# Softmax sums gathered by a chain of accumulating transfers, division on VectorE, and a new order at the start of each round

## The chip, the cores and the metric

The kernel runs on one core of a Trainium2 chip. The metric is the device time of one execution in microseconds (us). The engines are named as in the profile: PE is TensorE's matmul (PEld its weight load), DVE is VectorE, ACT is ScalarE, POOL is GpSimd, SP is SyncE.

## The reference

One transformer layer in float32 on `x` of 2 x 2048 x 512: a layer norm, attention with 16 query heads of 32 columns that share 2 key and value heads, and a linear layer in FP8. Cut to what matters here:

```python
x = x + attention(layernorm(x))
x = x + fp8_linear(layernorm(x), w_ffn)

def attention(x):
    q, k, v = x @ wq + bq, x @ wk + bk, x @ wv + bv   # 16, 2 and 2 heads of 32 columns
    q, k = rotary(q), rotary(k)
    scores = einsum('bqhd,bkhd->bhqk', q * hd**-0.5, repeat(k)) * hd**-0.5
    attn = softmax(scores, axis=-1)
    return einsum('bhqk,bkhd->bqhd', attn, repeat(v)).reshape(b, s, d) @ wo + bo
```

The softmax is exact: for each query and head the kernel needs the largest score, the sum of the exponentials over 2048 keys, and the values weighted by the exponentials, which are divided by that sum.

## The kernel before, in words

The tokens form 8 blocks of 512. A block's 16 heads are taken four at a time (a quad), and a quad's 512 queries in two halves of 256. One quad and half is a **unit**; there are 64, numbered `u`. The main loop runs over units, and in each over four **rounds** of four key chunks (128 keys each). In the text rounds are numbered 1 to 4 (`r` is 0 to 3 in the code).

Each round does two things at once. For the next unit it computes plain scores (`s`, queries on partitions, L517) and their maxima over the keys (DVE's reductions into `part`, L524). For this unit it computes transposed scores `T` (keys on partitions, L963; in round 1 the maxima come in ahead of them by the selector matmuls of L954), from which ACT makes the exponentials `p` (L972), and PE multiplies these with the values (`columns`, L913) into `avs[:, 0, :]`. Plain scores come in pairs, one for each call of `next(scores)`. The text calls the four pairs of a round a, b, c and d. PE's order in a round is: a, T of the first and second chunk, b, other work, T of the third, c, T of the fourth, other work, d, then the value matmuls of all four chunks, and in some rounds sums behind them.

PSUM has eight banks in use. Two tiles of two banks (`E` and `O`) hold `T` by turns. Three banks hold `s`, of which one is lent to other work (projections, output products, transposes) while such work is going on. One bank holds the tile `avs`: its first half are the weighted values of this unit, its second half the sums of the unit before.

The sums of the exponentials are made in two steps. On POOL `add_pair` (L946) adds the exponentials of two chunks; the round's first pair goes to a tile `pair`, its second to a tile of `far_sums`, and an accumulating transfer from POOL's queue (L1015) adds the first to the second. In round 3 one more transfer (L1017) adds the far sum of round 1 to that of round 2. So three tiles are left, and PE adds these over the partitions with a matrix of ones (`sum_up`, L927) into `avs[:, 1, :]` in the next unit: two tiles behind the values of round 1, one behind those of round 2. Each tile takes eight of the instructions that the profile counts.

Then `finish_heads` divides: ACT copies the sums from PSUM to the SBUF tile `both` (L885), DVE takes the reciprocals in two pieces (L889), and POOL multiplies them with the values (L890), which ACT had copied from `avs[:, 0, :]` to `both` at the unit's end (L1033).

Each engine works through its queue in the order in which the kernel writes it down. Around the fixed steps, `fill` hands out pieces of other work at set places: PE's pieces behind b and behind the fourth T, DVE's behind d. A list `finishing` goes ahead of the lists `queue` and `beside`. What a kind of step waits for is settled when the program is built: an instruction waits for a count of the engine or the transfer that it depends on.

Of the kernel before, what the change touches and what calls it, by code (L numbers as in the profile page):

```python
# [8 lines left out]
F32 = mybir.dt.float32  # L9
# [4 lines left out]
ALU = mybir.AluOpType  # L14
AX = mybir.AxisListType

P = 128
# [10 lines left out]
def preln_attn_fp8_ffn_kernel(  # L28
# [37 lines left out]
    nc = tc.nc  # L66
# [9 lines left out]
    HB = 256  # L76
# [6 lines left out]
    ON_PE, ON_DVE, OTHER = "PE", "DVE", "other"  # L83
# [9 lines left out]
    w2 = ctx.enter_context(tc.tile_pool(name="w2", bufs=6))  # L93
# [376 lines left out]
    units = [(k, half) for k in range(len(quads)) for half in range(HALVES)]  # L470
# [20 lines left out]
    def batch(k):  # L491
        return quads[k][0] // NB
# [267 lines left out]
    finishing = []  # L760
    attn_of = {}

    def fill(kind, pieces=1):

        for _ in range(pieces):
            ready = [job for job in queue if job.due <= step[0] and not job.waits()]
            if lent[0] is not None:
                ready = [job for job in ready if job is owner[0]]
            able = [
                (jobs, job)  # L770
                for jobs, some in ((finishing, finishing[:1]), (queue, ready), (beside, beside))
                for job in some
                if job.kind in (kind, OTHER) and job.due <= step[0]
            ]
            if able:
                do(*able[0])

    def do(jobs, job):
        held = lent[0]
        job.step()  # L780
        if held is None and lent[0] is not None:
            owner[0] = job
        if job.kind is None:
            jobs.remove(job)
# [93 lines left out]
            fetch_y_over_keys(4, "kS", 0)  # L878
            fetch_y_over_keys(5, "dkS", 0)

    def finish_heads(u, both, sums):

        k, half = units[u]
        n, quad = quads[k]
        nc.scalar.copy(both[:, 1, :], sums)  # L885
        for c in range(HB // P):
            yield ON_DVE
            piece = both[:, 1, c * P : (c + 1) * P]
            nc.vector.reciprocal(piece, piece)  # L889
        nc.gpsimd.tensor_tensor(  # L890
            attn_of[n][:, quad, half * HB : (half + 1) * HB], both[:, 0, :], both[:, 1, :], ALU.mult
        )
        if n == NBLK - 1:
            if quad == QUADS - 2 and half == HALVES - 1:
                queue.append(Job(finish_most(n, x_res[n], attn_of[n])))
            elif quad == QUADS - 1:
                queue.append(Job(finish_rest(n, x_res[n], attn_of[n], half)))
        elif quad == QUADS - 1 and half == HALVES - 1:
            job = Job(finish_block(n, attn_of.pop(n)))
            if n not in biased:  # L900
                job.due = NEVER
                without_x[n] = job
            queue.append(job)

    def columns(u, chunks, probs, av):

        k, half = units[u]
        for kc, p in zip(chunks, probs):
            if kc == NTS - 2 and u + 1 < len(units):
                tp = ps_t.tile([P, 4 * HB], F32, tag="E", name=f"mtp_{u + 1}")  # L910
                gather_maxima(u + 1, tp)
            for j in range(4):
                nc.tensor.matmul(  # L913
                    av[j * HD : (j + 1) * HD, :],
                    vX[batch(k)][:, kc, group(k), :],
                    p[:, j, :],
                    start=(kc == 0),
                    stop=(kc == NTS - 1),
                    tile_position=(0, j * HD),
                    skip_group_check=True,  # L920
                )

    def sum_up(dst, parts, start, stop):

# [12 lines left out]
    def add_pair(u, kc, a, b):  # L937
        far = kc % ROUND == 2
        pa = papool.tile(
            [P, 4, HB],  # L940
            F32,
            tag="pa" if far else "pair",
            name=f"pa_{u}_{kc}",
            bufs=4 if far else 2,
        )
        nc.gpsimd.tensor_tensor(pa, a, b, ALU.add)  # L946
        return pa

    def probabilities(u, T, kc):

        k, half = units[u]
        if kc < 2:
            for j in range(4):
                nc.tensor.matmul(  # L954
                    T[:, j, :],
                    sel[:, j, :],
                    maxima[u],
                    start=(j % 2 == 0),
                    stop=True,
                    skip_group_check=True,  # L960
                )
        for j in range(0, 4, 2):
            nc.tensor.matmul(  # L963
                T[:, j : j + 2, :],
                stacked["dkS"][:, group(k), kc * P : (kc + 1) * P],
                qst[k][:, j : j + 2, half * HB : (half + 1) * HB],
                start=False,
                stop=True,
                skip_group_check=True,
            )  # L970
        p = ppool.tile([P, 4, HB], F32, tag="p", name=f"p_{u}_{kc}")
        nc.scalar.activation(p, T, AF.Exp, scale=SCALE)  # L972
        return p

    with tc.manual_schedule():
        for _ in range(LEAD):
            next(scores)
        for u, (k, half) in enumerate(units):
            n, quad = quads[k]
            if half == 0 and quad == 0:  # L980
                attn_of[n] = wide.tile(
                    [P, QUADS, TB], F32, tag="attn", name=f"attn_{n}", bufs=2
                )
            stack_next(u)
            banks = [
                ps_t.tile([P, 4, HB], F32, tag="EO"[parity], name=f"T_{u}_{parity}")
                for parity in range(2)
            ]

            far_sums = []  # L990
            whole = u == len(units) - 1
            ending_soon = u >= len(units) - 2
            pieces = 2 if ending_soon else 1
            for r in range(ROUNDS):
                chunks = list(range(r * ROUND, (r + 1) * ROUND))
                step[0] += 1
                while r == 1 and landing:
                    landing.pop()()
                if r == 2:
                    ask(u)  # L1000
                last = r == ROUNDS - 1
                next(scores, None)
                probs = [probabilities(u, banks[kc % 2], kc) for kc in chunks[:2]]
                pair = add_pair(u, chunks[0], *probs)
                next(scores, None)
                if r > 0:
                    fill(ON_PE, pieces)
                probs.append(probabilities(u, banks[0], chunks[2]))
                next(scores, None)
                probs.append(probabilities(u, banks[1], chunks[3]))  # L1010
                if ending_soon:
                    fill(ON_DVE)
                if not (last and whole):
                    far_sums.append(add_pair(u, chunks[2], *probs[2:]))
                    nc.gpsimd.dma_start(out=far_sums[r], in_=pair, accum_op=ALU.add)  # L1015
                if r == 2:
                    nc.gpsimd.dma_start(out=far_sums[1], in_=far_sums[0], accum_op=ALU.add)  # L1017
                fill(ON_PE, pieces)
                next(scores, None)
                split_maxima()  # L1020
                fill(ON_DVE, 3 if finishing else 2)
                if r == 0:
                    avs = ps_av.tile([P, 2, HB], F32, tag="av", name=f"avs_{u}")
                columns(u, chunks, probs, avs[:, 0, :])


                if u > 0 and r == 0:
                    sum_up(avs[:, 1, :], far_before[1:3], False, False)
                elif u > 0 and r == 1:
                    sum_up(avs[:, 1, :], far_before[3:], False, True)  # L1030
                    finishing.append(Job(finish_heads(u - 1, both, avs[:, 1, :])))
            both = w2.tile([P, 2, HB], F32, tag="both", name=f"both_{u}", bufs=1)
            nc.scalar.copy(both[:, 0, :], avs[:, 0, :])  # L1033
            far_before = far_sums
        sums = ps_s.tile([P, TB], F32, tag=s_bank(), name="sums_last")[:, :HB]
        sum_up(sums, [pair, *probs[2:], *far_sums[1:]], True, True)
        finishing.append(Job(finish_heads(u, both, sums)))
        fetch_y_over_keys(2, "kS", 1)
        attending[0] = False
        for jobs in (finishing, queue, beside):  # L1040
            while jobs:
                jobs[0].step()
                if jobs[0].kind is None:
                    jobs.pop(0)
# [122 lines left out]
```

## Time and profile before

| | |
|---|---|
| median of 3 runs | 2333.02 us (2332.41 to 2335.74) |
| profiled execution, its own time | 2336.02 us |
| its span, first to last instruction | 2334.2 us |
| mean granted clock of TensorE | 0.97 |
| busy: PE, DVE, ACT, POOL | 92%, 73%, 53%, 76% |
| main loop, about 130 to 2215 us | 64 units of 28.3 to 41.5 us |
| rounds in it | mostly 6.8 to 9.4 us |
| accumulating transfers between SBUF tiles | 319 of 512 KB, 4.9 us to landing (median) |

The span has three parts: the projections of the first blocks (to about 130 us), the main loop, and the FP8 layer (from about 2235 us). A group's line gives the instructions' count, then busy time and mean ns of one, then the idle time of the engine just before them and what ended it. A line of the timeline gives start, length, engine, line, what is written and read, and in brackets how long the engine was idle before and who ended that. Where a line says "x4", four instructions are merged.

### The profile page before, as it was taken

The numbers are of one execution on the slowest core, as the hardware profiler recorded it, in microseconds if no ns is written. First come the engines' busy times: TensorE is split into PE (matmuls) and PEld (weight loads), VectorE is DVE, ScalarE is ACT, GpSimd is POOL, SyncE is SP. The second block draws the span as 40 slices with busy tenths as digits, with TensorE's granted clock in tenths as the row PEclk, the third lists the DMA queues.
The fourth block names the chain that finished last, engine by engine and source line by source line (L and its number), as shares of the span: only waits on it lengthen the run. The fifth ranks groups of instructions, "written<-read, shape, count | busy, mean of one in ns | idle before, by whom it ended". The sixth has DMA issues, their size and how long they took to land. (4 is left out here: it accounts for less than half of the span.)

```text
span 2334.2 us, 39403 instructions
## 1 busy us (share of the span) xinstructions
PE 2143.7 (92%) x15506; PEld 1242.2 (53%) x15506; DVE 1698.0 (73%) x2679; ACT 1237.0 (53%) x1545; POOL 1765.1 (76%) x1199
## 2 busy tenths in 40 slices
PE   5499999999999999999999999999999899899955
PEld 3255555555555555555555555555555455555522
DVE  3467778776777776876767778676877977767578
ACT  2146556655556555655445456555555555545646
POOL 3268889888878987888868878887888777877810
PEclk9599999999999999999999999999999999999978
DMA  6546656666465765659586456664665645847512
GB/s 204 160 102 128 141 114 161 140 142 131 100 163 130 159 129 136 145 115 197 103 202 137 102 127 136 147 112 96 133 154 123 138 101 115 170 98 197 109 52 112
DMA packets 116411, 312.78 MB, mean 134 GB/s; under 512 B 16896, under 2 KB 17536, under 8 KB 112384
## 3 DMA queue, kind: packets, MB, share of 16 engines
q0 software_dynamic: 50160, 175.66, 40.0%
q1 hardware_dynamic: 63648, 133.21, 19.2%
q8 instruction: 122, 2.00, 0.3%
q10 hardware_dynamic: 2416, 1.38, 0.2%
q14 instruction: 65, 0.53, 0.1%
HBM read 91.56 MB, written 42.99 MB: 58 GB/s over the span
## 5 line engine op out<-in xcount | busy, mean ns | idle before, releaser
L524 DVE TENSOR_REDUCE part<-s 128x1 f32<-128x512 f32 x2048 | 1304.2, 684 | 541.8 <-PE s L517 528.8
L946 POOL TENSOR_TENSOR pa<-p,p 128x1024 f32<-128x1024 f32 x511 | 1234.9, 2466 | 293.1 <-ACT p L972 265.8
L972 ACT ACTIVATE p<-T 128x1024 f32<-128x1024 f32 x1024 | 1001.4, 1024 | 597.8 <-PE T L963 564.6
L517 PE MATMUL s<-kS,qst 128*128 128x512 f32 x2048 | 832.1, 465 | 87.6 <-DVE part L524 28.7
L963 PE MATMUL T<-qst,dkS 128*128 128x512 f32 x2048 | 669.5, 423 | 11.8 <-ACT p L972 11.8
L517 PEld LDWEIGHTS s<-kS,qst 128*128 128x128 f32 x2048 | 369.7, 190 | 478.0 <-DVE part L524 266.5
L913 PE MATMUL avs<-p,vX 128*32 128x256 f32 x8192 | 509.4, 383 | 0.8 <-ACT p L972 0.8
L963 PEld LDWEIGHTS T<-qst,dkS 128*128 128x128 f32 x2048 | 366.0, 189 | 159.8 <-ACT p L972 54.8
L913 PEld LDWEIGHTS avs<-p,vX 128*32 128x32 f32 x8192 | 233.1, 109 | 214.4 <-issue 79.6
L1015 POOL DMA_DIRECT2D pa<-pa x255 | 224.2, 879 | 80.3 <-POOL pa L946 75.6
L301 PE MATMUL po<-wo_sb,attn 128*128 128x512 f32 x256 | 130.7, 596 | 1.3 <-POOL attn L890 1.3
L889 DVE RECIPROCAL both<-both 128x128 f32<-128x128 f32 x128 | 112.4, 920 | 11.2 <-ACT both L885 11.2
L301 PE MATMUL pq<-xnT_q,wq_sb 128*128 128x512 f32 x224 | 114.3, 592 | 0.0
L927 PE MATMUL avs<-pa,ones 128*32 128x256 f32 x1512 | 105.5, 382 | 5.5 <-DMA pa<-pa 5.5
L885 ACT COPY both<-avs 128x256 f32<-128x256 f32 x63 | 23.5, 372 | 132.8 <-PE avs L927 132.8
L890 POOL TENSOR_TENSOR attn<-both 128x256 f32<-128x256 f32 x64 | 85.2, 1331 | 5.9 <-DVE both L889 5.9
L954 PEld LDWEIGHTS T<-mT,sel 128*128 128x128 f32 x512 | 78.7, 190 | 13.6 <-ACT mT L546 1.9
L954 PE MATMUL T<-mT,sel 128*128 128x256 f32 x512 | 82.2, 283 | 1.1 <-ACT mT L546 1.1
L1017 POOL DMA_DIRECT2D pa<-pa x64 | 74.2, 1159 | 3.9 <-DMA pa<-pa 3.6
L927 PEld LDWEIGHTS avs<-pa,ones 128*32 128x32 f32 x1512 | 49.2, 111 | 38.6 <-DMA pa<-pa 6.0
L546 ACT CAST mT<-mtp 128x256 fp32r<-128x256 f32 x64 | 23.9, 373 | 84.0 <-PE mtp L542 84.0
L532 ACT CAST mrow<-mx 128x8 fp32r<-128x8 f32 x64 | 13.1, 205 | 93.5 <-DVE mx L531 93.5
(126 smaller groups left out, 1160.8 us busy)
## 6 DMA issues: line engine op xcount, KB each, us to landing
pa<-pa POOLq DMA_DIRECT2D x319, 512.0 KB, 4.9
qst<-q_far SPq DMA_DIRECT2D x128, 256.0 KB, 4.3
x_kv<-in_L_attn_x_dram SPq DMA_DIRECT2D x8, 1024.0 KB, 8.8
q_far<-hi_q SPq DMA_DIRECT2D x32, 256.0 KB, 4.4
q_far<-lo_q SPq DMA_DIRECT2D x32, 256.0 KB, 3.7
x_res<-in_L_attn_x_dram SPq DMA_DIRECT2D x8, 1024.0 KB, 8.2
x_res<-in_L_attn_bo_dram POOLq DMA_DIRECT2D x8, 1024.0 KB, 11.6
out_dram<-v SPq DMA_DIRECT2D x16, 512.0 KB, 2.8
```

What stands on the lines that cost most here:

```text
L301: nc.tensor.matmul(dst, lhs(c), rhs(c), start=(c == 0), stop=(c == chunks - 1))
L517: nc.tensor.matmul(s, qst[k][:, j, at : at + P], stacked["kS"][:, group(k), kb * TB : (kb + 1) * TB], start=True, stop=True,)
L524: nc.vector.tensor_reduce(part[:, i, j, kb : kb + 1], s, AX.X, ALU.max)
L889: nc.vector.reciprocal(piece, piece)
L890: nc.gpsimd.tensor_tensor(attn_of[n][:, quad, half * HB : (half + 1) * HB], both[:, 0, :], both[:, 1, :], ALU.mult)
L913: nc.tensor.matmul(av[j * HD : (j + 1) * HD, :], vX[batch(k)][:, kc, group(k), :], p[:, j, :], start=(kc == 0), stop=(kc == NTS - 1), tile ...
L927: nc.tensor.matmul(dst[j * HD : (j + 1) * HD, :], ones, part[:, j, :], start=start and i == 0, stop=stop and i == len(parts) - 1, tile_pos ...
L946: nc.gpsimd.tensor_tensor(pa, a, b, ALU.add)
L954: nc.tensor.matmul(T[:, j, :], sel[:, j, :], maxima[u], start=(j % 2 == 0), stop=True, skip_group_check=True,)
L963: nc.tensor.matmul(T[:, j : j + 2, :], stacked["dkS"][:, group(k), kc * P : (kc + 1) * P], qst[k][:, j : j + 2, half * HB : (half + 1) * H ...
L972: nc.scalar.activation(p, T, AF.Exp, scale=SCALE)
L1015: nc.gpsimd.dma_start(out=far_sums[r], in_=pair, accum_op=ALU.add)
```

## The change

Three things are changed.

1. The sums. The far sums of a unit are now added up by a chain of three transfers: round 1's into round 2's (issued in round 4), that into round 3's (in round 1 of the next unit), that into round 4's (in round 2 of the next unit). PE meets one tile instead of three, behind the values of round 3. The last two units that carry sums keep the earlier way (`in_one` is false).
2. The division. DVE takes the reciprocals in place in PSUM, in `avs[:, 1, :]`, and multiplies there by the values, which ACT copied to a tile of their own, `av`. ACT's copy of the sums and POOL's multiply are gone. The division's steps are handed out behind d of round 4 (of round 3 before), and `fill` gives four pieces there instead of three.
3. The order at a round's start: T of the first chunk, a, T of the second chunk, b.

```diff
-    def finish_heads(u, both, sums):
+    def finish_heads(u, av, sums):
 
         k, half = units[u]
         n, quad = quads[k]
-        nc.scalar.copy(both[:, 1, :], sums)
         for c in range(HB // P):
             yield ON_DVE
-            piece = both[:, 1, c * P : (c + 1) * P]
+            piece = sums[:, c * P : (c + 1) * P]
             nc.vector.reciprocal(piece, piece)
-        nc.gpsimd.tensor_tensor(
-            attn_of[n][:, quad, half * HB : (half + 1) * HB], both[:, 0, :], both[:, 1, :], ALU.mult
+        yield ON_DVE
+        nc.vector.tensor_tensor(
+            attn_of[n][:, quad, half * HB : (half + 1) * HB], av, sums, ALU.mult
         )
...
+    def in_one(u):
+
+        return 0 <= u < len(units) - 3
...
                 last = r == ROUNDS - 1
+                probs = [probabilities(u, banks[0], chunks[0])]
                 next(scores, None)
-                probs = [probabilities(u, banks[kc % 2], kc) for kc in chunks[:2]]
+                probs.append(probabilities(u, banks[1], chunks[1]))
                 pair = add_pair(u, chunks[0], *probs)
+
+                if last and not whole or r < 2 and in_one(u - 1):
+                    far, at = (far_sums, 1) if last else (far_before, r + 2)
+                    nc.gpsimd.dma_start(out=far[at], in_=far[at - 1], accum_op=ALU.add)
                 next(scores, None)
...
-                if r == 2:
+                if r == 2 and whole:
                     nc.gpsimd.dma_start(out=far_sums[1], in_=far_sums[0], accum_op=ALU.add)
                 fill(ON_PE, pieces)
                 next(scores, None)
                 split_maxima()
-                fill(ON_DVE, 3 if finishing else 2)
+                fill(ON_DVE, 4 if finishing else 2)
                 if r == 0:
                     avs = ps_av.tile([P, 2, HB], F32, tag="av", name=f"avs_{u}")
                 columns(u, chunks, probs, avs[:, 0, :])
 
 
-                if u > 0 and r == 0:
+                if u > 0 and r == 0 and not in_one(u - 1):
                     sum_up(avs[:, 1, :], far_before[1:3], False, False)
-                elif u > 0 and r == 1:
+                elif u > 0 and r == (2 if in_one(u - 1) else 1):
                     sum_up(avs[:, 1, :], far_before[3:], False, True)
-                    finishing.append(Job(finish_heads(u - 1, both, avs[:, 1, :])))
-            both = w2.tile([P, 2, HB], F32, tag="both", name=f"both_{u}", bufs=1)
-            nc.scalar.copy(both[:, 0, :], avs[:, 0, :])
+                    finishing.append(Job(finish_heads(u - 1, av, avs[:, 1, :])))
+            av = w2.tile([P, HB], F32, tag="av", name=f"av_{u}", bufs=1)
+            nc.scalar.copy(av, avs[:, 0, :])
             far_before = far_sums
```

In the changed program `sum_up`'s matmul is at L931, the chain's transfers at L1012, the pair's transfer at L1023, the reciprocals at L888 and the multiply at L890.

More of the change, by code (lines that the diff above doesn't have):

```diff
@@ L1036, in preln_attn_fp8_ffn_kernel @@
         sum_up(sums, [pair, *probs[2:], *far_sums[1:]], True, True)
-        finishing.append(Job(finish_heads(u, both, sums)))
+        finishing.append(Job(finish_heads(u, av, sums)))
         fetch_y_over_keys(2, "kS", 1)
```

## The prediction

> **What bounds the kernel now.** I read the page first, then the groups, the waits, the timeline of one unit, and the stretches in which PE stood still. A round's pairs of scores are called a, b, c, d, as in the section on the kernel.
>
> ```profile
> PE 2143.7 (92%) x15506; PEld 1242.2 (53%) x15506; DVE 1698.0 (73%) x2679; ACT 1237.0 (53%) x1545; POOL 1765.1 (76%) x1199
> ...
> PEclk9599999999999999999999999999999999999978
> ...
> L889 DVE RECIPROCAL both<-both 128x128 f32<-128x128 f32 x128 | 112.4, 920 | 11.2 <-ACT both L885 11.2
> ...
> L927 PE MATMUL avs<-pa,ones 128*32 128x256 f32 x1512 | 105.5, 382 | 5.5 <-DMA pa<-pa 5.5
> ...
> L890 POOL TENSOR_TENSOR attn<-both 128x256 f32<-128x256 f32 x64 | 85.2, 1331 | 5.9 <-DVE both L889 5.9
> ...
> L1017 POOL DMA_DIRECT2D pa<-pa x64 | 74.2, 1159 | 3.9 <-DMA pa<-pa 3.6
> ```
>
> PE is busy for 92% of the span and over 96% in the loop, so what PE's queue does in order sets a round's length. Its busy time contains small waits, and the waits view names the largest of them:
>
> ```profile
> PEld s L517 <- DVE part L524: 266.5, 668, 5.4
> POOL pa L946 <- ACT p L972: 265.8, 202, 12.6
> ```
>
> PE waits for DVE to free score banks; POOL has slack before its adds. Now the end of a round 3 and a round 4 of one unit, in the timeline (start, us):
>
> ```profile
> 404.39 1.75 DVE L889 RECIPROCAL both<-both 128x128 f32<-128x128 f32 x2
> ...
> 404.80 0.30 PEld L517 LDWEIGHTS s<-kS,qst 128*128 128x128 f32 x2 [0.41 <-DVE mx L531]
> ...
> 406.06 4.81 DVE L524 TENSOR_REDUCE part<-s 128x1 f32<-128x512 f32 x8
> ...
> 409.56 0.59 PEld L913 LDWEIGHTS avs<-p,vX 128*32 128x32 f32 x16 [0.25 <-issue]
> ```
>
> Two things are to be seen. The pair of reciprocals takes 1.75 us of DVE, and PE starts the next scores beside it. And the value matmuls (L913) of round 4 start at 409.56, while DVE finishes the last two reductions only at 410.87: PE does not wait for DVE there. Over 60 fourth rounds the last reduction ends 1.16 us (median; 0.80 to 1.32) after the first value weight load.
>
> Last, stretches around PE's longest stalls (PE busy is the first number after the length, the granted clock stands after POOL's count):
>
> ```profile
> 1196.40:1199.80 3.40, 1.17 (x24) 0.43 (x16) 2.26 (x4) 0.21 (x1) 3.10 (x3) 1.00 0.99 268
> 1199.80:1206.60 6.80, 6.17 (x13) 4.25 (x14) 2.58 (x4) 1.94 (x2) 4.32 (x5) 0.50 0.96 195
> 1466.00:1469.40 3.40, 1.88 (x34) 0.78 (x26) 0.97 (x2) 1.06 (x2) 3.19 (x5) 1.00 0.60 115
> 2036.10:2039.50 3.40, 1.34 (x28) 0.52 (x16) 0.27 (x2) 0.00 (x0) 0.35 (x1) 1.00 1.06 230
> 2039.50:2046.30 6.80, 3.34 (x20) 1.78 (x21) 0.64 (x2) 0.00 (x0) 5.29 (x3) 0.50 0.99 228
> ```
>
> The clock changes at steps of 3.4 us. Where PE was busy for 1.17 or 1.34 us of such a step, the clock was 0.50 in the next 6.8; at 1.88 us it stayed at 1.00.
>
> **The change, part by part.**
>
> *Sums.* From one start of L913 to the next round's a takes 2.73 us with sixteen sum instructions behind the values (388.83 to 391.56), 2.29 with eight (396.10 to 398.39), 1.86 with none (402.94 to 404.80). The change takes 0.87 from round 1 and 0.43 from round 2 and puts 0.43 into round 3: 0.87 us in each of 61 units, 53 us less for PE.
>
> *T of the first chunk ahead of a.* It adds no work, but the second score of b waits for DVE to have reduced a: a's weights at 592.45, that score's at 594.34 after a wait for DVE. With T (0.45 us in the timeline) ahead of a, DVE starts on a 0.45 later, and so does that score. I counted rounds by what held that score and the third T:
> - Round 1: in 27 of 60 the score was held and DVE was on time: 0.87 less for sums, 0.46 given back, 0.41 gained. In 15 without other PE work, where the third T waited for ACT, 0.14 is given back and 0.73 gained. In 12 DVE was late anyway and nothing is gained. Sum: −23 us (the other 6 shared out).
> - Round 2: 0.43 less 0.46 is nothing in the held rounds; 0.31 in 19 others. Sum: −5.
> - Round 3 becomes round 4's start: it bears the sums of round 3, and no reciprocals ahead of it. About 25 rounds lose 0.43, the others balance. Sum: +12.
> - Round 1's start, with four selector matmuls in each T: PE is late there as it is; 0.
>
> So of 53 us, 16 remain. The bounds are −53 (nothing given back) and +30 (0.46 in all 180 rounds 2 to 4, 83 − 53); I take −16, the row count.
>
> *The division on DVE from PSUM, and what waits for it.* This decides. In the list of instructions of the changed program the two reciprocals and the multiply stand in DVE's queue behind d's two reductions of round 4 (round 3 in the last two units), and the first value matmul of that same round waits for DVE's count that the multiply sets, in all 63 units that carry sums: values and sums are halves of one tile in one PSUM bank. In the kernel before only ACT's copy read the sums, a round earlier, and the reciprocals worked in SBUF, so no value matmul waited for them. PE is in order: behind the waiting matmul stand the value matmuls, the transposes of the maxima and the next round's T, and ACT, POOL and DVE wait for those. PE's wait per unit: 1.16 until the last reduction ends, 1.75 for two reciprocals, then the multiply, for which there is no row: the nearest is L573, 668 ns for 128x512 from PSUM, so 0.37 for half (between 0.35 and 0.67), and 0.05 to restart: 3.33 us. Bounds 2.85 (0.80 + 1.67 + 0.35 + 0.03) and 3.95 (1.32 + 1.90 + 0.67 + 0.06). Reciprocals in PSUM have no row; reductions take 0.68 from PSUM and 0.67 from SBUF, so I add nothing. 63 × 3.33 = +210 us (180 to 249). Nothing runs in that time that was late: the copy on ACT that goes (0.37) and the idle time of POOL were covered before.
>
> The Trainium skill ("PSUM — Partial Sum Buffer", section "PSUM bank collisions raise a hardware error") says that matmul writes and VectorE accesses to one bank and quadrant must be kept apart by semaphores, whatever the addresses. By that rule the wait belongs to the placing and couldn't be dropped; no run here shows a collision.
>
> *The clock.* A stall of 3.33 us falls on one or two steps of 3.4 us and takes at least 1.66 from one of them, which leaves PE about 1.7 us busy: between 1.34 (clock halved) and 1.88 (not). Most positions take more. So I expect half clock after nearly every one. Its price: the stall that ended at 2042.96 left 3.3 us at half clock, and the round that followed, from values to values, took 9.7 instead of 8.6: 1.1 us. The one ending near 1200.5 left 6.1 us, and two rounds took 22.3, against 17.4 in the neighbours, of which 2.9 were the stall: 2.0. Here half clock meets value matmuls, which nothing else hides. I take 1.3: 63 × 1.3 = +82; bounds 0 and 126.
>
> "TensorE: Matmul & The Clock Gate" in the skill (section "Why this matters for your kernels") warns of PE gaps above about 3 us and puts the fall of the clock on a window of idle. Read as a wholly idle window of its 3413 ns, a gap of 3.33 us would never do it and the clock's term would be 0; the rows with 1.17 and 1.34 us of work speak against that reading, and the sum goes by the rows.
>
> *Transfers.* 122 more issues at L1017's 0.86 to 1.16 us are 105 to 142 us of POOL, less 85 for L890: +20 to +57. Behind each issue in POOL's queue stand the round's second add, its transfer, the rotation's products and the split of the maxima. Cover: POOL's 265.8 us of waiting for ACT, and now 3 us of stall in each unit; uncovered it is the same 20 to 57. A link waits for the one issued a round (6.8 to 9 us) before; landing takes 4.7 and 6.8 us (medians of L1015 and L1017, 16.3 at most): 0, at worst 8 collisions with the bias transfers like the 5.5 us at L927. Software DMA goes from 40% to about 55% of the engines.
>
> *Tail.* The last division loses ACT's copy (0.37) and has the multiply at 0.37 instead of 1.33: −1.
>
> **Sum.** The profiled execution took 2336.0 us (span 2334.2 and 1.8 around it). 2336 − 16 − 1 + 210 + 82 = 2611. The median of the runs is 3 below that execution: 2608 us.
>
> **Rivals.**
> - *The clock stays up* (only the stall): 2336 − 3 − 17 + 210 = 2526. For it: 1.88 us of work kept the clock, and my 1.7 is near that. Chance 0.18.
> - *The clock stays down longer*, two steps after each stall, with the stall near its upper end: 63 × (3.7 + 2.0) = 359, nothing left of the gain: about 2690. For it: both 0.50 stretches above are 6.8 us long. Chance 0.15.
> - *Faster*: the value matmul finds the multiply done, since DVE does the division before d's reductions. Place: the end of round 4; it decides if DVE is free 2.1 us before PE reaches the values. Then 2333 − 17 = 2316, or 2279 if T first gives nothing back. Against it: DVE's order, and 1.16 us the other way in the median. Chance 0.03.
> - *No matter*: the wait is real but short, because DVE is ahead in longer rounds; about 17 us in all cancel the gain: 2333. That needs 0.27 us a unit where the shortest case gives 2.85. Chance 0.01.
>
> **How the numbers follow.** The forecast has 0.63, with its own range 2565 to 2650. The range 2515 to 2690 takes in the first two rivals' middles. A measurement tells about 0.2% (5 us) from no change. Faster 0.03, same 0.01, slower 0.96.
>
> **What would show it.** Right: a wait of PE at L913 for DVE's multiply L890, 63 times and about 3.3 us each, none of it at L913 before; half clock in the loop; L931 with 61 × 8 + 2 × 24 = 536 instructions where L927 had 1512. Wrong: L913 waiting less than 1 us, or clock 1.00 throughout the loop; then a time below 2530 would tell that the clock's term was too large, and one below 2330 that the division lies beside other work.

## The result and the profile after

The changed kernel takes 2664.8 us (median of four runs, 2658.2 to 2667.2); the kernel before took 2332.7 us beside it. The ratio is 1.142, with a 95% interval of 1.139 to 1.145: slower by 332 us. The profiled execution took 2665.7 us, its span is 2663.9 us, and the mean granted clock of TensorE fell from 0.97 to 0.92.

First the page of the changed kernel: the busy time of the engines, the granted clock in 40 slices, and three groups of instructions.

```profile
PE 2244.5 (84%) x14530; PEld 1258.2 (47%) x14530; DVE 1747.1 (66%) x2743; ACT 1226.9 (46%) x1481; POOL 1824.4 (68%) x1257
...
PEclk9699998999999999999999999999989889998878
...
L913 PE MATMUL avs<-p,vX 128*32 128x256 f32 x8192 | 588.6, 427 | 228.3 <-DVE attn L890 218.9
...
L1012 POOL DMA_DIRECT2D pa<-pa x185 | 167.9, 907 | 39.1 <-DMA pa<-pa 38.9
...
L888 DVE RECIPROCAL avs<-avs 128x128 f32<-128x128 f32 x126 | 121.1, 961 | 7.1 <-PE avs L931 4.9
```

The row of the value matmuls on the page of the kernel before:

```profile
L913 PE MATMUL avs<-p,vX 128*32 128x256 f32 x8192 | 509.4, 383 | 0.8 <-ACT p L972 0.8
```

PE is busy for 84% instead of 92%. The value matmuls (L913) did not wait for DVE before; now PE stands in front of them for 218.9 us. They also became dearer: the same 8192 matmuls are busy for 588.6 us where they took 509.4. That difference of 79 us is where the lower clock is seen best.

The row of the clock shows this badly: a 9 stands for anything from 0.9, and a slice of 67 us holds two stalls and two stretches at half clock of a few us each. The windows view, cut along one stall, shows it.

The waits view of the changed kernel (total us, times, longest):

```profile
PEld s L517 <- DVE part L524: 349.2, 863, 5.7
ACT mT L546 <- PE mtp L542: 341.1, 64, 6.3
PEld avs L913 <- DVE attn L890: 243.1, 62, 4.0
PE avs L913 <- DVE attn L890: 218.9, 62, 3.7
```

The wait is met 62 times, 3.53 us each, and never lasts over 3.7 us. The line on ACT is its echo: the transposed maxima stand behind the first half of these value matmuls in PE's queue, so ACT's copy of them waited 341 us, where it waited 84 before. The first line grew too, from 266.5 us: the other order at a round's start does this (356.1 us in the run of the order alone, below).

One stall in the timeline (start, us, engine):

```profile
553.11 4.88 DVE L524 TENSOR_REDUCE part<-s 128x1 f32<-128x512 f32 x8 [1.72 <-PE s L517]
...
557.90 1.96 DVE L888 RECIPROCAL avs<-avs 128x128 f32<-128x128 f32 x2
...
559.90 0.42 DVE L890 TENSOR_TENSOR attn<-av,avs 128x256 f32<-128x256 f32 x1
...
560.37 0.20 PEld L913 LDWEIGHTS avs<-p,vX 128*32 128x32 f32 x8 [3.94 <-DVE attn L890]
560.37 1.93 PE L913 MATMUL avs<-p,vX 128*32 128x256 f32 x16 [3.62 <-DVE attn L890]
```

The bracket says that PE had been idle for 3.62 us, so since 556.75. The parts can be read off: 1.15 until the reciprocals start, 1.96 for the two, 0.42 for the multiply, and 0.09 for the gaps between.

And the windows around this stall and an earlier one (length, then busy time of PE, PEld, DVE, ACT and POOL, then the granted clock):

```profile
447.70:451.10 3.40, 1.60 (x6) 0.87 (x5) 3.09 (x6) 2.04 (x2) 3.40 (x3) 0.99 0.42 80
451.10:454.50 3.40, 1.58 (x16) 0.59 (x16) 1.69 (x3) 0.00 (x0) 2.43 (x2) 0.51 0.73 140
454.50:457.90 3.40, 3.40 (x25) 1.52 (x22) 0.00 (x0) 0.75 (x2) 0.10 (x1) 0.50 0.82 153
...
557.00:560.40 3.40, 0.03 (x4) 0.03 (x5) 3.33 (x6) 0.14 (x1) 3.40 (x3) 1.00 0.28 53
560.40:563.80 3.40, 3.40 (x30) 1.34 (x34) 1.74 (x1) 0.37 (x1) 3.10 (x3) 0.50 0.80 153
```

In the last two rows the step with the stall is granted full speed while PE stands; the next one, in which the value matmuls run, gets half. There the stall fills one step almost wholly. It need not: the stall that ended at 452.92 lay over the border of two steps and left PE 1.60 us of work in the first, and the clock fell behind it. The second, with 1.58 us, ran at half already, and the step behind it did too. Counted over the main loop, 66 such stretches, 41 of 3.4 us and 25 of 6.8, add up to 311 us at 0.50. They come with 58 of the 62 stalls. The other four also lay over a border and met no half clock; the one near 904 us left PE 1.73 and 1.61 us of work. A unit without other work grew from 28.4 to about 33 us.

### The profile page after: what moved, and what is told of

The parts are those of the page before. It is cut to its first block, busy times and chain, and to the rows that moved or that the text cites. A ratio compares the mean times of both kernels' runs of the same rounds, so it can differ in the third digit from the quotient of the medians.

```text
span 2663.9 us, 37611 instructions
## 1 busy us (share of the span) xinstructions
PE 2244.5 (84%) x14530; PEld 1258.2 (47%) x14530; DVE 1747.1 (66%) x2743; ACT 1226.9 (46%) x1481; POOL 1824.4 (68%) x1257
## 3 DMA queue, kind: packets, MB, share of 16 engines
q1 hardware_dynamic: 63648, 133.21, 16.9%
## 4 chain that ended last, share of the span: by engine, by line
PE 52%; DVE 26%; DMA 8%; POOL 5%; ACT 4%; issue 3%; SPq 0%; DVEq 0%; ACTq 0%; POOLq 0%
PE avs L913 16%; DVE part L524 15%; PE s L517 12%; PE T L967 11%; DMA pa<-pa 6%; DVE avs L888 4%; POOL pa L950 4%; PE po L301 4%; PE pq L301 3%; PE T L958 3%; ACT p L976 3%; DVE sw_q L319 2%; PE mtp L542 1%; PE avs L931 1%; DVE attn L890 1%
## 5 line engine op out<-in xcount | busy, mean ns | idle before, releaser
L950 POOL TENSOR_TENSOR pa<-p,p 128x1024 f32<-128x1024 f32 x511 | 1273.4, 2504 | 420.6 <-ACT p L976 403.1
L517 PE MATMUL s<-kS,qst 128*128 128x512 f32 x2048 | 843.2, 463 | 93.1 <-DVE part L524 32.1
L913 PE MATMUL avs<-p,vX 128*32 128x256 f32 x8192 | 588.6, 427 | 228.3 <-DVE attn L890 218.9
L967 PE MATMUL T<-qst,dkS 128*128 128x512 f32 x2048 | 723.6, 436 | 2.7 <-ACT p L976 2.7
L517 PEld LDWEIGHTS s<-kS,qst 128*128 128x128 f32 x2048 | 393.9, 193 | 461.5 <-DVE part L524 349.2
L913 PEld LDWEIGHTS avs<-p,vX 128*32 128x32 f32 x8192 | 248.7, 118 | 482.9 <-DVE attn L890 243.1
L1023 POOL DMA_DIRECT2D pa<-pa x255 | 223.8, 878 | 82.8 <-POOL pa L950 72.2
L1012 POOL DMA_DIRECT2D pa<-pa x185 | 167.9, 907 | 39.1 <-DMA pa<-pa 38.9
L888 DVE RECIPROCAL avs<-avs 128x128 f32<-128x128 f32 x126 | 121.1, 961 | 7.1 <-PE avs L931 4.9
L247 POOL TENSOR_TENSOR lo_q<-q,hi_q 128x512 fp32r<-128x512 f32 x32 | 41.1, 1283 | 100.0 <-ACT hi_q L246 99.9
L319 DVE SCALAR_TENSOR_TENSOR sw_q<-sw_q,sign,cs 128x512 f32<-128x512 f32 x30 | 63.8, 2127 | 0.7 <-issue 0.5
L301 PEld LDWEIGHTS po<-wo_sb,attn 128*128 128x128 f32 x256 | 49.1, 192 | 12.8 <-issue 3.4
L1101 PE MATMUL py<-wT,xqT 128*128 128x512 bf16 x128 | 44.3, 482 | 10.8 <-ACT xqT L1093 10.8
```

The lines of the kernel that those rows point to most:

```text
L301: nc.tensor.matmul(dst, lhs(c), rhs(c), start=(c == 0), stop=(c == chunks - 1))
L319: nc.vector.scalar_tensor_tensor(t[:rows], t[:rows], sign[:rows], csb[:rows, 1, :], ALU.mult, ALU.mult)
L517: nc.tensor.matmul(s, qst[k][:, j, at : at + P], stacked["kS"][:, group(k), kb * TB : (kb + 1) * TB], start=True, stop=True,)
L913: nc.tensor.matmul(av[j * HD : (j + 1) * HD, :], vX[batch(k)][:, kc, group(k), :], p[:, j, :], start=(kc == 0), stop=(kc == NTS - 1), tile ...
L967: nc.tensor.matmul(T[:, j : j + 2, :], stacked["dkS"][:, group(k), kc * P : (kc + 1) * P], qst[k][:, j : j + 2, half * HB : (half + 1) * H ...
L1012: nc.gpsimd.dma_start(out=far[at], in_=far[at - 1], accum_op=ALU.add)
```

## The experiments

The questions were how the 332 us divide over the three parts of the change, whether the half clock costs what the prediction charged for it, and, after the first runs, why the chain of transfers saves nothing. Every kernel below was timed beside the kernel before, which took 2333.1 us beside the first four and 2332.5 us beside the last four.

### The division alone

The kernel before with only the division of the changed one: reciprocals and multiply on DVE from PSUM, in round 3.

```diff
-        nc.scalar.copy(both[:, 1, :], sums)
...
-            piece = both[:, 1, c * P : (c + 1) * P]
+            piece = sums[:, c * P : (c + 1) * P]
...
-        nc.gpsimd.tensor_tensor(
-            attn_of[n][:, quad, half * HB : (half + 1) * HB], both[:, 0, :], both[:, 1, :], ALU.mult
+        yield ON_DVE
+        nc.vector.tensor_tensor(
+            attn_of[n][:, quad, half * HB : (half + 1) * HB], av, sums, ALU.mult
...
-                fill(ON_DVE, 3 if finishing else 2)
+                fill(ON_DVE, 4 if finishing else 2)
```

> The kernel before with only the division changed: reciprocals and multiply on DVE in PSUM, three tiles met by PE as before, old order at a round's start. Theory 1: 63 waits of L913 for the multiply, now at the end of round 3, about 3.5 us each, and half clock after nearly each: 2333 + 63 x 3.5 + 63 x 1.3 to 1.6 = 2635 to 2655 us. Rival 2: within 20 us of 2333.

Measured: 2621.7 us, ratio 1.1235 (1.1213 to 1.1256), so +289 us. From its waits:

```profile
PE avs L913 <- DVE attn L890: 227.4, 62, 3.9
PEld s L517 <- DVE part L524: 213.7, 585, 3.1
```

The division alone brings the whole wait, and 289 of the 332 us, 13 us less than the least that was expected. The second line is shorter than before (266.5): after a stall DVE has caught up with the reductions, and PE's later scores wait 53 us less for their banks. This fits the fact that the stall (227) and the clock (measured below in the whole change, about 104) add up to more than 289.

### The division away from the shared bank

The changed kernel, in which ACT first copies the sums to SBUF, and DVE divides there.

```diff
+        held = w2.tile([P, HB], F32, tag="held", name=f"held_{u}", bufs=1)
+        nc.scalar.copy(held, sums)
+        sums = held
         for c in range(HB // P):
```

> The changed kernel with one difference: ACT copies the sums from PSUM to an SBUF tile as soon as PE has written them, and DVE's reciprocals and multiply work there. The chain, the new order and DVE's multiply stay. Theory 1 (the division in the values' PSUM bank holds up PE, and the clock falls after each hold-up): the wait of L913 for DVE's multiply is gone, the granted clock is back at 0.96 to 0.97, and the time is that of the first forecast without its two large terms, about 2316 us (2295 to 2345). Rival 2 (the chain's 122 more transfers and the new order make the loss, and PE would have waited elsewhere): over 2500 us still, with POOL or DMA named in the waits.

Measured: 2411.9 us, ratio 1.0337 (1.0320 to 1.0354). The wait at L913 is gone, and with it 253 us, so these are paid for the division's use of the tile that the values are written to. Whether sums in a bank of their own would do as well is not shown: no run gives them one. And 79 us stay above the kernel before, which was not expected. The largest new wait is not on PE (ACT's copy of the values, whose tile the multiply reads late), and DVE's multiply takes longer here, with both operands in SBUF, than the 421 ns of the changed kernel:

```profile
ACT av L1044 <- DVE attn L893: 115.3, 57, 4.6
```

```profile
L893 DVE TENSOR_TENSOR attn<-av,held 128x256 f32<-128x256 f32 x64 | 60.7, 949 | 2.2
```

Behind the wait of ACT come waits for the transfers: 38.6 and 35.0 us on POOL, 30.6 us on PE. The next two runs ask whether the 79 us are in the order or in the chain; they give 37 each, 74 together. What the longer multiply costs was not separated.

### The order alone

The kernel before with T of the first chunk ahead of a.

```diff
+                probs = [probabilities(u, banks[0], chunks[0])]
                 next(scores, None)
-                probs = [probabilities(u, banks[kc % 2], kc) for kc in chunks[:2]]
+                probs.append(probabilities(u, banks[1], chunks[1]))
```

> The kernel before with only the order at a round's start changed: transposed scores of the first chunk ahead of the first pair of plain scores. My count of rounds (0.46 us given back in 57 rounds 2 and 3 whose second score of b was held by DVE, 0.14 in 34 others, little where DVE was late): 2333 + 31 = 2364 us (2340 to 2395). Rival: the earlier first exponential takes the third T's wait for ACT away (45.9 us of it) and the adds on POOL start earlier: 2300 to 2333 us.

Measured: 2370.3 us, ratio 1.0153 (1.0134 to 1.0172), so +37 us. PE's weight loads in one round of this kernel's timeline:

```profile
590.27 0.30 PEld L963 LDWEIGHTS T<-qst,dkS 128*128 128x128 f32 x2 [0.41 <-issue]
590.62 0.42 PEld L517 LDWEIGHTS s<-kS,qst 128*128 128x128 f32 x2
...
592.62 0.19 PEld L517 LDWEIGHTS s<-kS,qst 128*128 128x128 f32 x1 [0.41 <-DVE part L524]
```

The round of the kernel before that the prediction read:

```profile
592.45 0.30 PEld L517 LDWEIGHTS s<-kS,qst 128*128 128x128 f32 x2 [0.41 <-issue]
...
594.34 0.19 PEld L517 LDWEIGHTS s<-kS,qst 128*128 128x128 f32 x1 [0.41 <-DVE part L524]
```

T comes first, and the second score of b, which waits for DVE, comes 2.35 us after the round's start; it came 1.89 after it before. The difference is 0.46 us, the time of one T, as the prediction had it.

### The chain alone

The kernel before with the chain of transfers and PE's one tile; the division stays on SBUF copies, in round 4, with a second buffer for the copies.

```diff
+                if last and not whole or r < 2 and in_one(u - 1):
+                    far, at = (far_sums, 1) if last else (far_before, r + 2)
+                    nc.gpsimd.dma_start(out=far[at], in_=far[at - 1], accum_op=ALU.add)
...
-                if u > 0 and r == 0:
+                if u > 0 and r == 0 and not in_one(u - 1):
                     sum_up(avs[:, 1, :], far_before[1:3], False, False)
-                elif u > 0 and r == 1:
+                elif u > 0 and r == (2 if in_one(u - 1) else 1):
...
-            both = w2.tile([P, 2, HB], F32, tag="both", name=f"both_{u}", bufs=1)
+            both = w2.tile([P, 2, HB], F32, tag="both", name=f"both_{u}", bufs=2)
```

> The kernel before with only the sums changed: chain of transfers, one tile met by PE behind round 3, division as before on copies in SBUF (handed out behind round 4's d, with two buffers for the copies), old order. Theory 1: 0.87 us less of PE in each of 61 units, most of it kept: 2280 to 2300 us. Rival 2: POOL's issues (20 to 57 us net of nothing here, since POOL keeps its multiply: 105 to 142) or late links cost more than that: 2335 to 2400 us.

Measured: 2369.6 us, ratio 1.0157 (1.0130 to 1.0184): +37 us, where a gain was expected. Its waits:

```profile
ACT p L976 <- POOL pa L950: 94.9, 46, 8.2
...
POOL pa L950 <- DMA pa<-pa: 40.5, 21, 4.8
...
PE avs L931 <- DMA pa<-pa: 34.0, 10, 5.7
```

Before, PE waited 5.5 us for these transfers, and ACT less for POOL:

```profile
ACT p L972 <- POOL pa L946: 28.1, 19, 4.6
```

On POOL the links themselves (L1011) wait another 27.4 us, in 11 places. How a late link reaches PE is seen in one unit's timeline:

```profile
527.04 0.84 POOL L1011 DMA_DIRECT2D pa<-pa  x1
...
538.45 0.87 POOL L1011 DMA_DIRECT2D pa<-pa  x1 [4.55 <-DMA pa<-pa]
...
539.06 2.63 POOL L950 TENSOR_TENSOR pa<-p,p 128x1024 f32<-128x1024 f32 x1
...
541.72 1.94 ACT L976 ACTIVATE p<-T 128x1024 f32<-128x1024 f32 x2 [5.29 <-POOL pa L950]
...
544.29 0.79 PE L517 MATMUL s<-kS,qst 128*128 128x512 f32 x1 [5.27 <-ACT q L450]
```

The link issued at 527.04 had not landed until shortly before 538.45; between 524.76 and 532.79 SP had issued eight transfers for the next queries and other tiles. The next link reads what the first one writes, so POOL stood for 4.55 us with the second add of the round behind it. ACT's exponentials waited for that add (their tile is free when it is done), and PE for ACT's step at L450, which stands behind the exponentials. One late transfer costs all four engines about 5 us (DVE stood for 5.37 before 545.12). A link that is issued later still was not tried.

Such waits also lower the clock. From 130 us to the last value matmul PE stood idle for 82 us before and for 143 with the chain alone, while its busy time fell by 25 us (2010 to 1985) and not by the prediction's 53. The trace of the chain alone has 19 stretches at half clock there, 96 us in all; that of the kernel before has 4, 24 us. At the price that *Work in PE's wait* gives (104 us for 311 us at half clock reduced to 44), the 72 us more cost about 28. That is an estimate; it is as large as the part of the gain that is missing.

### The load of the transfers alone

The kernel before with 122 more accumulating transfers of 512 KB, issued at the links' places. They go to a DRAM tile that nothing reads, so no one waits for their sums; only POOL's adds wait now and then until a transfer has read its tile (8 times, 11.0 us in all).

```diff
+                if r < 2 and 0 < u < len(units) - 2:
+                    aside = dram.tile([P, 4, HB], F32, tag=f"aside_{r}_{u % 2}", name=f"aside_{u}_{r}")
+                    nc.gpsimd.dma_start(out=aside, in_=far_before[r + 1], accum_op=ALU.add)
```

> The kernel before with 122 more accumulating transfers of 512 KB on POOL's queue at the places of the chain's links in rounds 1 and 2, each from a far sum to a DRAM tile that nobody reads; the sums are as before. It measures load and issue without PE or POOL waiting for what lands (but for the reuse of the far sums a round later). Theory A (waits for late links make the chain's loss): 2333 + 10 to 30 = 2343 to 2363 us. Theory B (load and issue make it): 2333 + 80 to 100 = 2413 to 2433 us.

Measured: 2363.0 us, ratio 1.0129 (1.0114 to 1.0144), so +30 us for issue and load. These transfers write DRAM and the chain's write SBUF, so this is a neighbour of the chain's load, not the same thing. The chain alone costs 37 more than nothing after a gain in PE that the prediction put at 53: about 90 in all. Taking the 30 for load, some 60 are left for links that are late, the half clock behind them included.

### One more link instead of two

The kernel before, with one more link for each unit (two, where the chain has three) in place of one of PE's three tiles, and its result read a round later.

```diff
+                if r == 1 and u > 0:
+                    nc.gpsimd.dma_start(out=far_before[3], in_=far_before[2], accum_op=ALU.add)
...
-                    sum_up(avs[:, 1, :], far_before[1:3], False, False)
-                elif u > 0 and r == 1:
+                    sum_up(avs[:, 1, :], far_before[1:2], False, False)
+                elif u > 0 and r == 2:
...
-            both = w2.tile([P, 2, HB], F32, tag="both", name=f"both_{u}", bufs=1)
+            both = w2.tile([P, 2, HB], F32, tag="both", name=f"both_{u}", bufs=2)
```

> The kernel before with half a chain: one more transfer per unit (round 3's sum into round 4's, issued in round 2 of the next unit), which does not wait for a link of the round before it, and two tiles met by PE instead of three, behind rounds 1 and 3. Theory A (the chain alone lost because links that wait for a link block POOL's queue when loads delay them): 0.43 us less of PE in 63 units, 27 us, less about 10 of POOL: 2310 to 2325 us. Theory B (each added transfer costs by its load and issue, 122 of them about 90 us): 2333 - 27 + 45 = 2350 us.

Measured: 2319.1 us, ratio 0.9943 (0.9925 to 0.9961). This version beats both kernels, by 13 us the one before. It takes eight sum instructions from each unit, 63 × 0.43 = 27 us by the prediction's row, and keeps half of that. If a transfer more costs half of the 30 us that two cost above, the other half is accounted for. Here ACT waits 19.2 us for POOL's adds, less than the 28.1 before.

### Work in PE's wait

The changed kernel with 13 matmuls that nothing reads ahead of the values of round 4, in 61 units. They fill the wait without shortening it, so what the time loses is the price of the clock.

```diff
+                if r == 3 and in_one(u - 1):
+                    idle = ps_t.tile([P, 4, HB], F32, tag="E", name=f"idle_{u}")
+                    for _ in range(13):
+                        nc.tensor.matmul(
+                            idle[:, :2, :],
+                            stacked["kS"][:, group(k), :P],
+                            qst[k][:, :2, :HB],
+                            start=True,
+                            stop=True,
+                            skip_group_check=True,
+                        )
                 columns(u, chunks, probs, avs[:, 0, :])
```

> The changed kernel with thirteen more matmuls of 128x512 between d and the values of round 4, in 61 units. They write into the idle T bank, nothing reads them, and they take about 13 x 0.23 = 3.0 us of PE, less than PE's wait for the multiply (3.5 us). So the wait itself is as long as before and only PE's idleness goes. Theory 1 (half clock after each wait has a price of its own, forecast at 1.3 us): granted clock back at 0.96 to 0.97 and 61 x 1.0 to 2.0 us less than the changed kernel: 2540 to 2605 us. Rival (the wait is the whole price, or the halved clock hides beside other engines): 2655 to 2675 us.

Measured: 2560.8 us, ratio 1.0973 (1.0951 to 1.0994) to the kernel before, and 104 us less than the changed kernel. The mean granted clock is back at 0.97, with 44 us at half clock in the main loop in place of 311. What is left of the wait, and the value matmuls:

```profile
PE avs L913 <- DVE attn L890: 34.2, 58, 3.7
```

```profile
L913 PE MATMUL avs<-p,vX 128*32 128x256 f32 x8192 | 512.9, 384 | 42.4 <-DVE attn L890 34.2
```

PE still waits a little after the added matmuls, so they ended before the division did. More work, and the kernel is faster: 104 / 61 = 1.7 us for each unit is the price of half clock after a stall. Of it 76 us are in the value matmuls (588.6 to 512.9).

### The division behind the values

The changed kernel, with the division's steps handed out behind the values of round 4 and not ahead of them.

```diff
-                fill(ON_DVE, 4 if finishing else 2)
+                late, behind = finishing[:], 0
+                if r == ROUNDS - 1 and late:
+                    finishing.clear()
+                    behind = 3
+                fill(ON_DVE, 1 if behind else 4 if finishing else 2)
...
                 columns(u, chunks, probs, avs[:, 0, :])
+                if behind:
+                    finishing.extend(late)
+                    fill(ON_DVE, behind)
```

> The changed kernel with the division handed out behind the values of round 4 instead of ahead of them (still on DVE in PSUM). Theory 1 (the wait comes from the order of the two users of the bank): L913 does not wait for the multiply any more and the clock stays up; DVE now begins the division only when the values are done, some 0.3 us after its last reduction, and is 2.3 us late for the next round's a, of which PE feels 0.5 to 1.5 us in each unit: 2407 (the sum of the order alone and the chain alone, both measured) plus 30 to 90 = 2435 to 2500 us. Rival (any division in the values' bank holds PE up for as long): over 2600 us.

Measured: 2451.6 us, ratio 1.0511 (1.0495 to 1.0527). Of the value matmuls' wait for the division 3.7 us are left, and 213 us are gone. The shared tile still costs, in the other direction:

```profile
PE s L517 <- DVE part L524: 82.2, 94, 5.4
...
DVE avs L888 <- PE avs L913: 50.0, 48, 2.3
```

DVE now waits for the values before it divides, and the reductions of the next round stand behind it; PE's scores wait for these 82.2 us, where it was 32.1 in the changed kernel.

## Why the prediction was right, and where it was off

The sign, the cause and the size of the largest part were as predicted: the value matmuls of round 4 wait for DVE's division because sums and values share a tile, and nearly each wait (58 of 62) brings half clock. The profiled execution was put at 2611 and took 2666, 55 more; the median was put at 2608 and is 2665. That lies inside the range, and 15 us above the forecast's own range of 2565 to 2650. Step by step:

| step | predicted, us | measured, us | from |
|---|---|---|---|
| division: PE's wait | +210 | 62 × 3.53 = 219 in the trace | waits, changed kernel |
| clock | +82 | 104 | work in PE's wait |
| both together | +292 | +289 | division alone |
| order (the part of *Sums* that T gives back) | +37 | +37 | order alone |
| *Sums* and *Transfers* together | −53 + 0 | +37 | chain alone |

**Division.** The wait was built from 1.16, 1.75, 0.37 and 0.05. The stall shown above has 1.15, 1.96, 0.42 and 0.09: the reciprocals and the multiply were each a little dearer than the rows taken for them, which were of SBUF or of another shape. The count was right within one (62 against 63), and L931 has the 536 instructions that were stated.

**Clock.** 1.3 us was taken for each stall, between rows of 1.1 and 2.0; the runs showed 1.7. The rivals in which the clock stays up (2526) or stays down for two steps each time (about 2690) are excluded by the granted clock, which fell for one step in 41 of 66 cases and for two in 25, and by the added matmuls. As stall and clock were each set too low, it is luck in part that their sum is right: the prediction held that nothing late runs in the stalls, and PE gets some 42 us of them back (227 in the run of the division alone, and the 104, less 289). DVE's reductions being ahead after a stall fits that, and is argued from one line of the waits, not shown.

The prediction weighed a rule of the Trainium skill here ("TensorE: Matmul & The Clock Gate", section "Why this matters for your kernels"). Its warning of gaps above about 3 us holds for 58 of the 62 stalls. Its window of idle, read as a wholly idle one, does not: a step with 1.60 us of work was followed by half clock, as the rows with 1.17 and 1.34 us had suggested. No sharp border shows: a step with 1.61 us was not.

**Order.** Counting rounds by what held the second score and the third T gave 37 us, and the run gave 37. The same count, made again for the order alone, gave 31, so the exact match is luck; the way of counting held.

**Transfers: the step that failed.** It was put at 0, at worst 44, from medians of landing (4.7 and 6.8 us) against the distance of one round (6.8 to 9 us). Alone, the chain costs about 90, if the gain of 53 is real: 30 for issue and load, and about 60 for links that are late, of which some 28 are half clock. In the whole change, 332 − 289 − 37 leaves 6 for the chain, so −53 and +59 in this way of counting. This is the missing 57 us of the median. The step named the right collision (a transfer that takes longer than a round), but priced it by the one engine that had shown it, PE at L927, and by 8 cases. A late link also holds POOL, and through POOL's add ACT and PE, and where PE stands for long, the clock falls.

The three parts alone add up to 289 + 37 + 37 = 363 us, and the whole is 332. So 31 us are saved by the parts being together. In the changed kernel PE waits less for transfers than with the chain alone (11.8 us against 34.0), and ACT less for POOL (53.2 against 94.9), while POOL's links wait more (38.9 against 27.4) and its adds less (16.9 against 40.5). This fits stalls that give the links time. That this is all of the 31 us is not shown, nor is the division of the chain's 37 into gain, load and lateness, which leans on the prediction's 53 for the gain.

## What to carry to other kernels

Before an operation is moved to read PSUM in place, ask who writes that tile next and how far behind the reader stands in its own queue: a copy of 0.37 us on an engine with slack was what kept 3.5 us of waiting, and mostly half clock after it, off PE here. A transfer that the next one depends on has to be given the time of its slow tail, not of its median, and its price is that of every engine whose queue stands behind the wait. When a saving is cut into three steps, trying one of them may be worth more than all: one more link for each unit gained 13 us, two more lost 37.

## What was not expected of the hardware

- A stall of 3.5 us on PE cost another 1.7 us by the granted clock, and 61 × 13 matmuls without any use made the kernel 104 us faster. The clock fell behind a step of 3.4 us that was only half idle (1.60 us of work), and came back late: in the changed kernel's main loop, steps at half clock with up to 2.94 us of work were followed by another at half, those with 2.96 us and more by full speed.
- A 512 KB accumulating transfer between SBUF tiles landed in about 5 us in the median (5.2 for the links of the chain alone, 4.9 in the changed kernel), but one link took over 11 us (issued at 527.04, landed shortly before 538.45) in a stretch with eight issues by SP around it.
- The reciprocal of 128x128 took 961 ns in PSUM and 920 in SBUF; the multiply of 128x256 took 421 ns with one operand in PSUM, and 949 with both in SBUF.
